# Opening the accumulators of layer 2's feed-forward by a flag instead of by products of zeros

## The chip, the cores and the metric

The kernel runs on one core of one Trainium2 chip. A core has several engines that each work through a queue of their own, in order: TensorE (PE in the profile; PEld is its weight load), VectorE (DVE), ScalarE (ACT), GpSimd (POOL) and SyncE (SP), which here issues DMAs. They meet only through semaphores. The metric is the device time of one execution in microseconds; of several runs the median is taken.

## The reference

The reference is a network of four layers on 16 sequences of 128 tokens with 128 features; each layer is an attention followed by a feed-forward, each added to x. The change lies in the feed-forward of layer 2, a product-key mixture of 1024 small experts:

```python
xn = _rmsnorm(x, norm_w)
q = (xn @ w_q.T).reshape(b, t, H, 2, DK)
sim1 = jnp.einsum('bthd,hkd->bthk', q[..., 0, :], keys[:, :, 0, :])
sim2 = jnp.einsum('bthd,hkd->bthk', q[..., 1, :], keys[:, :, 1, :])
s1, i1 = jax.lax.top_k(sim1, K)
s2, i2 = jax.lax.top_k(sim2, K)
all_idx = (i1[..., :, None] * NKEYS + i2[..., None, :]).reshape(b, t, H, K * K)
all_sc = (s1[..., :, None] + s2[..., None, :]).reshape(b, t, H, K * K)
fs, pk = jax.lax.top_k(all_sc, K)
fi = jnp.take_along_axis(all_idx, pk, axis=-1)
wd = expert_down[fi]
wu = expert_up[fi]
hidden = jax.nn.gelu(jnp.einsum('btd,bthkd->bthk', xn, wd), approximate=False)
hidden = hidden * jax.nn.relu(fs)
return jnp.einsum('bthk,bthkd->btd', hidden, wu)
```

There are H = 8 heads, 32 keys in each of two halves, and K = 8 experts are chosen per head. An expert is a pair of keys, so each token has a grid of 32 x 32 = 1024 sums of similarities per head, and the eight largest of them are wanted with their places.

## The kernel before

**No gather.** The kernel does not fetch the chosen experts. It computes the gelu for all 1024 experts and multiplies it with a weight for every expert, which is zero for those not chosen. The weight is built by subtraction. For each head the full grid C of sums is made; the eight largest are replaced in it by 0; the sum over the heads of the whole grid minus the sum of the grids with the holes leaves just the chosen sums. Both terms are gathered in one accumulator pc in PSUM, with the sign turned and turned back at the end.

**Tiles.** A tile is one sequence, 128 tokens; there are 16 (`NB`), in groups of four (`GB`). The function `layer2_ffn` is a generator whose inner functions are the steps of a tile:

- `begin(n)`, once a group: root mean square norm, transposes, `xT`, and `tT`, the similarities summed over the heads, features by tokens.
- `similar(i)`: the product psim of a tile with all keys (line 1415 copies it to `sim`).
- `thresholds(sim)`: DVE finds the eight best of each half (`best`, line 1424), POOL adds them pairwise (`sums`, line 1429), DVE finds the eight best of these (`m8`, line 1436), ACT takes relu (`out`, line 1440).
- `grid(sim, h)`: POOL adds the two halves into the 32 x 32 grid C of a head (line 1447; eight buffers C). For head 4 (`own`) ACT makes the grid row by row instead (`rows`, line 1456; buffers Cs).
- `opened(i)`: takes a new accumulator pc, two banks of 512 columns, from `ps2` (three such pairs, shared with pg of this feed-forward and pe of the attention). PE first multiplies zeros into each bank, `none` against `none`, 128 x 512 in bf16, with the start flag. Then eight products of the selection matrix `sel` with `tT` add minus the full sums, each into 128 columns, four of them per bank, without the start flag. A product of fp32 stands as two records in the profile.
- `taken(pc, h, C, m8)`: DVE searches the head's grid and puts zeros at the eight largest (line 1475), then PE transposes the grid in eight pieces onto pc (line 1477), adding.
- `gelus(i)`: PE makes pg, ACT its gelu G (line 1406).
- `weighted(pc, G)`: DVE multiplies -pc by G (line 1485), when all eight heads are in.
- `summed(i, A)`: PE multiplies G with the up-projection into po, and DVE adds it to X (line 1494).

The products made by the helper `mm` all carry line 232 in the profile, so they are told apart by their tile names; the same holds for transposes through `transposed` (line 293).

**What sets the order.** For each tile the loop writes: `opened(i)`, then for heads 0 to 7 the next tile's grids, rows and part of its thresholds and `taken`; `summed(i - 1)` stands after head 2, `gelus(i)` after head 4, `similar(i + 2)` after head 6; `weighted` ends the tile. The function `layers_1_and_2` takes one piece of this generator and one piece of the attention of layer 2 for the last two groups in turn (`chains`), so that both run side by side. In that attention line 1249 to 1263 is the softmax, line 1282 and 293 are transposes of x and E, and line 245 is the reciprocal root on POOL (`rstd`) behind which ACT scales (`low`, line 270, and x or xn, line 274). The written order is only the wish: the framework fills each engine's queue at build time by a planner that, with costs of its own for every instruction, takes among those that it believes ready the one written first. Semaphores and buffers are assigned afterwards; on the chip every queue then runs strictly as filled.

Of the kernel before, what the change touches and what calls it, by code (L numbers as in the profile page):

```python
# [19 lines left out]
P = 128  # L20
# [161 lines left out]
def build(ctx: ExitStack, tc: tile.TileContext, x, ctxt, mask, packs, cols, out):  # L182
# [45 lines left out]
    def ps2(name):  # L228
        return pss.tile([P, 2, 512], F32, tag="s", name=name)

    def mm(o, lhsT, rhs, start=True, stop=True):
        return nc.tensor.matmul(o, lhsT=lhsT, rhs=rhs, start=start, stop=stop)  # L232
# [1123 lines left out]
    def layer2_ffn(wk):  # L1356
# [8 lines left out]
        none = wk.tile([P, 512], BF16, name="none", bufs=1)  # L1365
# [94 lines left out]
        def opened(i):  # L1460

            n, b = divmod(i, GB)
            tT = group[n][1][:, b * P : (b + 1) * P]
            pc = ps2("pc")
            for r in range(2):
                mm(pc[:, r, :], none[:, :P], none, start=True, stop=False)
            for k in range(8):
                mm(pc[:, k // 4, k % 4 * P : (k % 4 + 1) * P], w["sel"][:, k * P : (k + 1) * P], tT,
                   start=False, stop=False)
            return pc  # L1470

        def taken(pc, h, C, m8):
# [39 lines left out]
        for i in range(NB):  # L1512
            pc = opened(i)
            if i % GB == 1 and i + GB < NB:
                begin(i // GB + 1)
            if i + 1 < NB:
                pieces = thresholds(sims[i + 1])
            for h in range(8):
                at = 8 * i + h + 4
                if at < 8 * NB and at % 8 != own:  # L1520
                    Cs[at] = grid(sims[at // 8], at % 8)
                if i + 1 < NB:
                    if h == 0:
                        Cs[8 * i + 8 + own] = slow()
                    rows(sims[i + 1], Cs[8 * i + 8 + own], h)
                taken(pc, h, Cs.pop(8 * i + h), m8)
                if h == 2 and last is not None:
                    summed(i - 1, last)
                if h == 4:
                    G = gelus(i)  # L1530
                if h == 6 and i + 2 < NB:
                    sims[i + 2] = similar(i + 2)
                if i + 1 < NB:
                    later = next(pieces)
                yield
            last, m8 = weighted(pc, G), later
# [171 lines left out]
```

## Time and profile before

| | us |
|---|---|
| median of 3 runs | 1429.53 |
| lowest and highest | 1420.95, 1430.63 |
| the profiled execution | 1422.77 |
| its span, from first to last instruction | 1421.0 |
| PE busy in the span | 1174.5 (83%) |
| DVE busy | 866.8 (61%) |
| ACT busy | 701.1 (49%) |
| POOL busy | 466.6 (33%) |
| mean granted clock of TensorE | 0.898 |
| 32 products of zeros, first and last start | 908.8, 1226.5 |

Times in a profile row are counted from the start of the span. A row of a group gives the line, the engine and operation, what is written from what is read, the shapes and how many there were; then the busy time and the mean of one in ns; then the idle time of the engine just before them, and who ended it. A row of the waits names who waited, for whom, the sum in us, the number of waits and the longest. A row of the order of time gives start and length in us, engine, line and operation, and in brackets the idle time before it. A row of the chain gives start, length and what ran. "issue" is time for which no waiting is seen. The length of a product includes its way through the pipeline, so two products in a row overlap; the step from one start to the next is what a product costs PE.

### The profile page before, as it was taken

Reading aid. Unit: us, or ns where it says so; the run is one execution under the profiler, and the core shown is the slowest. Engines: PE = TensorE matmul, PEld = TensorE weight load, DVE = VectorE, ACT = ScalarE, POOL = GpSimd, SP = SyncE. Lnnn points to the kernel's source line nnn. Section 1 sums busy time; section 2 is a strip of 40 time slices with the busy share of each in tenths; the row PEclk is TensorE's granted clock in tenths of the full one; section 3 lists DMA queues with packets and bytes.
Section 4 is the critical chain, followed back from the end, with each engine's and each line's share of the span. In section 5 each row is a group of like instructions: output and inputs, shape, how many; then the busy total and the mean of one; then the engine's idle time right before and its main releaser. Section 6 shows DMA issues by size and latency. Waiting matters only on the chain. (4 is left out here: it accounts for less than half of the span.)

```text
span 1421.0 us, 25103 instructions
## 1 busy us (share of the span) xinstructions
PE 1174.5 (83%) x9948; PEld 793.1 (56%) x9948; DVE 866.8 (61%) x2249; ACT 701.1 (49%) x1519; POOL 466.6 (33%) x543
## 2 busy tenths in 40 slices
PE   5887799898998877987778387568989999979996
PEld 2445355454544423455557266447868888825465
DVE  7666456565655585666554431237867999775653
ACT  4444465564665332565534146348768675334331
POOL 3213000000000045554230400229867899641100
PEclk9998799999999967899879588769999999999997
DMA  7000000000000020000012112000000000000001
GB/s 232 2 2 19 0 0 1 0 1 0 1 1 0 13 100 1 2 2 2 2 39 70 58 42 100 12 0 1 1 2 1 5 6 2 1 7 1 2 2 30
DMA packets 27590, 27.09 MB, mean 19 GB/s; under 512 B 3408, under 2 KB 25808, under 8 KB 27088
## 3 DMA queue, kind: packets, MB, share of 16 engines
q1 hardware_dynamic: 22128, 22.08, 4.7%
q0 software_dynamic: 1024, 2.10, 0.5%
q10 hardware_dynamic: 4320, 1.31, 0.4%
q8 instruction: 78, 1.28, 0.3%
q14 instruction: 40, 0.33, 0.1%
HBM read 17.88 MB, written 7.60 MB: 18 GB/s over the span
## 5 line engine op out<-in xcount | busy, mean ns | idle before, releaser
L1447 POOL TENSOR_TENSOR C<-sim 128x1024 f32<-128x1024 f32 x112 | 211.4, 1913 | 26.8 <-PE pc L1477 12.5
L232 PE MATMUL pc<-hm,weights_f 128*128 128x512 f32 x320 | 148.3, 595 | 3.0 <-DVE hm L840 2.6
L245 POOL TENSOR_TENSOR rstd<-ve,minus_half 128x4 f32<-128x4 f32 x44 | 44.9, 1020 | 292.7 <-DVE ve L242 275.4
L1475 DVE MATCH_REPLACE8 C<-out,C 128x1024 f32<-128x1024 f32 x112 | 135.0, 1208 | 0.0
L461 DVE TENSOR_REDUCE nm<-s 128x8 f32<-128x1024 f32 x96 | 114.2, 1217 | 21.2 <-PE s L232 20.5
L1477 PE MATMUL pc<-consts,C 128*128 128x128 f32 x896 | 115.9, 278 | 7.3 <-DVE C L1475 6.7
L1456 ACT ACTIVATE Cs<-sim 128x32 f32<-128x32 f32 x512 | 113.8, 310 | 1.5 <-PE pc L1477 1.2
L1477 PEld LDWEIGHTS pc<-consts,C 128*128 128x128 f32 x896 | 103.6, 144 | 15.1 <-issue 8.1
L525 DVE RECIPROCAL inv<-av 128x128 f32<-128x128 f32 x48 | 45.9, 957 | 89.0 <-PE av L232 89.0
L354 POOL MEMSET V<- 128x2560 f32 x6 | 13.4, 2258 | 248.7 <-PE pb L934 236.2
L605 ACT ACTIVATE pT<-st 128x1024 f32<-128x1024 f32 x64 | 62.3, 1022 | 66.0 <-PE st L232 66.0
L232 PEld LDWEIGHTS pc<-hm,weights_f 128*128 128x128 f32 x320 | 59.9, 190 | 55.5 <-issue 45.9
L232 PE MATMUL st<-Qb,K 32*128 32x512 f32 x512 | 82.8, 651 | 0.0
L232 PE MATMUL s<-Kb,Q 32*128 32x512 f32 x384 | 74.7, 679 | 6.5 <-ACT pT L533 2.9
L535 POOL TENSOR_TENSOR E<-pT 128x1024 f32<-128x1024 f32 x32 | 60.5, 1907 | 55.7 <-ACT pT L533 55.7
L475 POOL CAST nms<-nm 128x16 bf16<-128x16 f32 x64 | 14.6, 255 | 157.1 <-DVE nm L461 132.6
L232 PEld LDWEIGHTS av<-pT,V 128*32 128x32 f32 x1536 | 43.2, 117 | 40.4 <-issue 26.3
L533 ACT ACTIVATE pT<-st 128x1024 f32<-128x1024 f32 x32 | 31.4, 1022 | 61.6 <-PE st L232 61.5
L232 PE MATMUL av<-pT,V 128*32 128x128 f32 x1536 | 58.5, 294 | 1.6 <-DVE inv L549 1.2
L840 DVE TENSOR_TENSOR hm<-he,M 128x512 f32<-128x512 f32 x64 | 40.8, 686 | 29.9 <-ACT he L836 27.1
L232 PE MATMUL av<-pT,consts 128*32 128x128 f32 x1536 | 54.4, 283 | 0.0
L603 ACT ACTIVATE pT<-st,keys_out 128x1024 f32<-128x1024 f32 x32 | 33.9, 1111 | 37.1 <-PE st L232 37.1
(370 smaller groups left out, 2674.7 us busy)
## 6 DMA issues: line engine op xcount, KB each, us to landing
weights_f<-in_f SPq DMA_DIRECT2D x1, 3852.5 KB, 12.0
weights_f<-in_f SPq DMA_DIRECT2D x1, 2816.5 KB, 9.7
rows<-zero SPq DMA_DIRECT2D x2, 1344.0 KB, 14.9
of<-rows SPq DMA_DIRECT2D x14, 192.0 KB, 2.5
outs<-rT SPq DMA_DIRECT2D x14, 192.0 KB, 2.0
weights_f<-in_f SPq DMA_DIRECT2D x1, 2351.5 KB, 11.2
X<-in_x ACTq DMA_DIRECT2D x4, 256.0 KB, 9.5
ctx_sb<-in_ctx SPq DMA_DIRECT2D x4, 256.0 KB, 5.8
```

The source lines that it names most:

```text
L232: return nc.tensor.matmul(o, lhsT=lhsT, rhs=rhs, start=start, stop=stop)
L245: nc.gpsimd.tensor_tensor(o, ve, minus_half[:, :w], ALU.pow)
L461: nc.vector.tensor_reduce(nm[:, b, 8 * u : 8 * u + 8], ss[u].rearrange("p r (g k) -> p (r g) k", g=4), AX.X, ALU.max, negate=True,)
L525: nc.vector.reciprocal(y, s)
L535: nc.gpsimd.tensor_mul(E2, E, E)
L603: nc.scalar.activation(pT, st, AF.Exp, bias=keep[1][:, i : i + 1])
L605: nc.scalar.activation(pT, st, AF.Exp)
L840: nc.vector.tensor_mul(hm[:, k, c : c + 2, :], he, M[:, k, c : c + 2, :])
L1447: nc.gpsimd.tensor_add(C, sim[:, h, 0, :].unsqueeze(2).to_broadcast(sh), sim[:, h, 1, :].unsqueeze(1).to_broadcast(sh),)
L1456: nc.scalar.activation(C[:, k, :], sim[:, own, 1, :], AF.Identity, bias=sim[:, own, 0, k : k + 1])
L1475: nc.vector.match_replace(at, m8[:, h, :], at, 0.0)
L1477: nc.tensor.matmul(pc[:, k // 4, k % 4 * P : (k % 4 + 1) * P], lhsT=C[:, 4 * k : 4 * k + 4, :].rearrange("p i j -> p (i j)"), rhs=ident, s ...
```

## The change

In `opened`, the loop with the two products of zeros is removed. The first of the four selection products of each bank (k = 0 and k = 4) now carries the start flag; the other six go on without it. The tile `none` and the memset that fills it stay in the program, without a reader.

```diff
             pc = ps2("pc")
-            for r in range(2):
-                mm(pc[:, r, :], none[:, :P], none, start=True, stop=False)
             for k in range(8):
                 mm(pc[:, k // 4, k % 4 * P : (k % 4 + 1) * P], w["sel"][:, k * P : (k + 1) * P], tT,
-                   start=False, stop=False)
+                   start=k % 4 == 0, stop=False)
             return pc
```

## The prediction

> **What bounds the kernel now.** I first asked what the engines do in the stage that the diff touches. The table of busy time by stretch answers it (columns: PE, PEld, DVE, ACT, POOL busy with instruction counts, then granted clock, DMA share, GB/s):
>
> ```profile
> 1120.00:1160.00 40.00, 36.53 (x285) 33.53 (x286) 36.35 (x120) 30.07 (x115) 32.06 (x20) 0.96 0.03 9
> 1160.00:1200.00 40.00, 39.57 (x336) 37.28 (x335) 39.84 (x118) 24.55 (x98) 38.17 (x22) 1.00 0.01 2
> 1200.00:1240.00 40.00, 36.86 (x317) 34.91 (x315) 32.47 (x92) 14.18 (x53) 30.42 (x18) 1.00 0.00 1
> ```
>
> Three engines are nearly full at once: from 1160 to 1200 us PE 39.6, DVE 39.8 and POOL 38.2 of 40 us. Busy shares alone can't say what a shorter PE is worth here; the waits must.
>
> Next the waits, for all engines from 960 to 1240 us:
>
> ```profile
> DVE m L1436 <- POOL sums L1429: 12.6, 9, 5.2
> POOL C L1447 <- PE pc L1477: 12.5, 14, 2.4
> ...
> PE pt L1282 <- ACT x L274: 7.5, 5, 3.1
> ...
> PE po L232 <- DVE G L1485: 3.6, 3, 2.3
> ```
>
> Both directions occur: POOL waits for PE to free a buffer C (12.5 us in 14 waits), and PE waits for ACT (the attention's x) and for DVE's G. So PE is the late engine in some places and early in others. PE's order of time around a tile opening shows both:
>
> ```profile
> 1195.32 1.04 PE L1477 MATMUL pc<-consts,C 128*128 128x128 f32 x8
> 1196.20 0.59 PE L232 MATMUL pc<-none 128*128 128x512 bf16 x2
> 1196.63 1.95 PE L232 MATMUL pc<-tT,weights_f 128*128 128x128 f32 x16
> 1198.41 2.78 PE L1477 MATMUL pc<-consts,C 128*128 128x128 f32 x24
> 1203.46 2.05 PE L232 MATMUL po<-weights_f,G 128*128 128x128 f32 x16 [2.26 <-DVE G L1485]
> ...
> 1218.24 2.05 PE L232 MATMUL po<-weights_f,G 128*128 128x128 f32 x16 [0.88 <-DVE G L1485]
> ...
> 1226.28 0.59 PE L232 MATMUL pc<-none 128*128 128x512 bf16 x2
> ```
>
> The first row is the last eight transposes of tile 12; opening of tile 13 follows without a gap, then 24 transposes, and then PE stands 2.26 us for G of tile 12, although that tile's pc was complete at about 1196.2. G was simply late in DVE's queue. PE time saved between 1196 and 1201 therefore lengthens this wait and nothing else.
>
> Last, the chain that ended last. It can be followed back only to 1053 us; its pieces with an opening in them are
>
> ```profile
> 1080.52 0.65 PE pc L232 x4
> ...
> 1082.57 1.56 PE pc L232 x14
> ...
> 1196.36 2.22 PE pc L232 x18
> ...
> 1226.45 2.21 PE pc L232 x18
> ```
>
> That is three of the eleven openings after 1053 us. The other eight lie beside longer DVE, POOL or ACT work.
>
> **The change part by part.** *Removed:* two products of zeros per tile, 32 in all. The duration shown (379 ns) includes the pipeline; what counts is the step to the next start. The pair starts at 1196.20 and the first selection product at 1196.63: 0.43 us, and 0.44 at 1226.28 against 1226.72. Sixteen pairs are 16 x 0.433 = 6.9 us of PE, the most that the removal can give directly. Their weight loads (98 ns each) are beside PE.
>
> How much lies on the path? After 1053 us three openings: 3 x 0.43 = 1.3 us. The one at 1196 is doubtful (the wait at 1203 absorbs it on PE; POOL runs on without a gap), so 0.9 to 1.3. The last one is safe: from 1218.24 PE has no further gap until 1239, while POOL's last C has ended at 1230.4 and DVE stands 5.8 us for its last G. Before 1053 us the chain is not shown. Tile 0 opens at 908.8 and its first transpose starts only at 967.7, so its pair is worth nothing; the four openings from 980 to 1037 I take at the rate of the others, 3 in 11: 4 x 0.27 x 0.43 = 0.5 us (bounds 0 and 1.7). Sum: 1.3 + 0.5 = **1.8 us**; bounds with the order of instructions kept: 0.4 (only the last tile) and 6.9.
>
> *Moved:* the flag, and with it the wait for a free pair of banks, from the first product of zeros to the first selection product. No opening in the stage shows idle time ahead of it, so nothing queues behind that wait. A selection product's load (191 ns) now follows a transpose instead of a 216 ns product. The nearest row is the gelu product set behind transposes (1190.06 x8, then 1190.93: 0.87 us, 109 ns a piece, no gap), so I take 0; if the cover were gone, 191 - 109 = 0.08 us per tile, 1.3 us in all. Below nothing isn't possible, since the order of loads and products stays. The tile of zeros itself and its one memset (519 ns on POOL) stay.
>
> *A rule that speaks against it.* Work taken from PE just ahead of a wait makes PE's idle longer. Rows: from start to start PE stood 3.33 us until 1121.05, and the clock of 1118 to 1126 was 0.79; it stood 2.69 us until 1143.22 and 2.53 until 1203.46, and both stretches show 1.00. With 0.43 added the latter two become 3.1 and 3.0 us. The Trainium skill, "TensorE: Matmul & The Clock Gate", section "Why this matters for your kernels", advises against PE gaps over about 3 us, its section on what is happening gives a free-running window of about 3.4 us. By the rule's short figure both gaps may drop the clock, for one window: half of 3.4, so 1.7 us each, 3.4 us, more than the gain. By the rows and the window's length neither does (longest unpunished 2.69, punished 3.33, mine between). I take 0 because 3.0 and 3.1 are under the window, and keep 1.7 to 3.4 us for the range.
>
> *The order.* Each engine's queue is filled at build time by a planner which takes what it believes is ready. The diff changes that belief from the first opening on. DVE's G of tile 12 stands behind seven searches of tile 13, that of tile 3 behind one, so positions do move. A G one search earlier is 1.19 us earlier (searches 1212.27 and 1213.46); PE waited for G in four of the last tiles for 4.1 us, so a luckier plan can give up to that. An unluckier one is the rival below. Neither is in the trace; I take 0 and keep both ends.
>
> The profiled execution: span 1421.0, its own time 1422.77 (1.8 around the span). 1422.77 - 1.8 = 1421.0. But it lies 6.8 below the median of the three runs, 1429.53 (1420.95 to 1430.63); on the median the same saving gives 1429.53 - 1.8 = **1427.7 us**. The runs' own spread of 9.7 us is five times what I expect, so only many rounds could show it; 1% of the time, 14.3 us, is about what a measurement of this kernel can tell from no change.
>
> **The rivals.**
>
> *PE is the bound throughout.* For: PE idles almost nothing between 1144 and 1187 us, with tiles 13.64 us apart. Against: DVE is at 39.8 of 40 us there, and PE's waits for G follow. It gives 6.9: 1422.6 us. With a luckier order of G (up to 4.1 more) it reaches 1418.5.
>
> *Hidden wholly.* Only the last tile's 0.4 counts: 1429.1. For: eight of eleven openings are off the chain. It sits inside my own case.
>
> *Slower: a reshuffled POOL queue.* The two attention chains that run beside the tiles pass through POOL ten times for rstd:
>
> ```profile
> L1447 POOL TENSOR_TENSOR C<-sim 128x1024 f32<-128x1024 f32 x101 | 190.8, 1914 | 26.0 <-PE pc L1477 12.5 <-issue 5.0 <-PE pe L232 4.5
> L245 POOL TENSOR_TENSOR rstd<-ve,minus_half 128x4 f32<-128x4 f32 x10 | 10.4, 1035 | 2.6 <-ACT ve L240 1.9 <-PE pc L1477 0.7
> ```
>
> With PE believed earlier, a C buffer seems free earlier, and the planner sets one more grid C (1.87 us from start to start) ahead of an rstd. Behind an rstd stand ACT's low and x and then PE, which is in order: ACT low waits for rstd 11.1 us in 7 waits already. Price: 1.87 us for each rstd that falls behind one C more, at most 10 x 1.87 = 18.7 us. From the first that isn't made up, 1.87 - 1.8, the change no longer gains; from nine (16.8 - 1.8 = 15.0) it is over 1% slower. Half of them, my price for this case: 9.4 - 1.8 = 7.6, so 1437 us. Against it: the same shift can as well put a C behind an rstd. More table loads on ACT (1.28 us) I exclude: four loads for the exponentials and four for gelu stand beside four groups of exponentials, so they are already fully interleaved.
>
> *It doesn't do what it says.* Were the flagged product to clear only its own 128 columns, old sums would stay and the output would be wrong, at the same time of 1427.7. No trace shows this; "PSUM — Partial Sum Buffer", "The four PSUM rules", says that the flag clears the whole bank's marks, so the three unflagged products overwrite.
>
> **How the numbers follow.** Own case (0.4 to 3 us gained, order about as now) 0.55; full gain, with or without luck, 0.15; slower order 0.27, of which over 1% slower 0.1; a much luckier order of the chains 0.03. The range takes own case, full gain and most of the slower one, with the runs' spread (their low end 8.6 below the median): 1416 to 1438. Within 1% are 1415.2 to 1443.8: faster 0.05, same 0.83, slower 0.12.
>
> **What would show it.** Right: no pc from zeros; first selection product directly behind a transpose at 0.11 us; tiles in the full stretch near 13.2 us on PE but not on DVE or POOL; PE's wait for G longer (above 4.1 us); PE's last G some 0.4 to 3 us earlier in the span. The PE rival: tiles 13.2 us apart, with no more waiting for G. The slower one: ACT low's wait for rstd well above 11.1 us, and the attention ending later than 1145 us. Clock drops near 1143 or 1203 would show the rule. I am wrong if stages before 900 or after 1250 us move by more than the stage itself, or if the planner's new order moves more than 5 us.

## The result and the profile after

The change made the kernel slower: median 1434.49 us (1429.12 to 1443.36, 14 runs) against 1427.7 us before (1420.95 to 1431.33, 14 runs). The ratio is 1.0065, with a 95% interval of 1.0046 to 1.0084: between 6.6 and 12.0 us lost. It is within 1%, and inside the range, but on the other side of the 1.8 us that were forecast as a gain. All times of tiles and stretches below come from one profiled execution of each kernel; a ratio comes from many runs, each kernel against the kernel before in the same rounds. (The prediction took 1% as about the least that could be told from no change; these runs tell 0.65%.)

The products of zeros are gone (9916 records of products instead of 9948), and the profiled execution's span grew from 1421.0 to 1429.8 us. The page's first lines after the change:

```profile
span 1429.8 us, 25054 instructions
## 1 busy us (share of the span) xinstructions
PE 1174.3 (82%) x9916; PEld 794.5 (56%) x9916; DVE 864.4 (60%) x2249; ACT 703.1 (49%) x1521; POOL 465.9 (33%) x543
```

PE's busy time hardly fell (1174.5 to 1174.3) although 32 products are missing. So others must have become longer, which points at the clock: from 972 us to the end of the stage the mean granted clock is 0.99 before and 0.96 after. To find where the time went I read the start of each tile's first selection product in both traces, and cut the stage at these starts. The stage runs from the product pk with the keys (937.3 us before, 939.2 after) to the last product po (1242.5 and 1253.4):

| stretch | before | after |
|---|---|---|
| start of the stage (pk) to the last po | 305.3 | 314.2 |
| pk to tile 0 | 20.0 | 19.8 |
| tile 0 to tile 6 | 123.5 | 121.2 |
| tile 6 to tile 7 | 19.7 | 27.0 |
| tile 7 to tile 9 | 36.7 | 36.2 |
| tile 9 to the last po | 105.3 | 110.1 |
| behind the last po | 178.4 | 176.4 |

Up to tile 6 the change gains 2.3 us, which is near the forecast; but the kernel with all its zeros in the new order (below) takes 121.5 us there too, and the change in the old order 123.1, so these 2.3 us aren't the saved products. Then tile 6 alone takes 7.3 us more, and the last six tiles take 4.8 us more. The edit moves the lines behind it: what is line 1477 (transposes), 1475 (searches) and 1485 (G) in the kernel before is 1475, 1473 and 1483 after the change, and 1478, 1476 and 1486 in the first run below. This is POOL's order of time in that tile, first before, then after (start, length, engine, line, operation, and in brackets the idle time before it):

```profile
1085.14 1.92 POOL L1447 TENSOR_TENSOR C<-sim 128x1024 f32<-128x1024 f32 x1 [2.39 <-PE pc L1477]
1087.01 1.02 POOL L245 TENSOR_TENSOR rstd<-ve,minus_half 128x4 f32<-128x4 f32 x1
1088.00 3.78 POOL L1447 TENSOR_TENSOR C<-sim 128x1024 f32<-128x1024 f32 x2
```

```profile
1086.68 5.66 POOL L1447 TENSOR_TENSOR C<-sim 128x1024 f32<-128x1024 f32 x3 [2.18 <-PE pc L1475]
1092.29 1.02 POOL L245 TENSOR_TENSOR rstd<-ve,minus_half 128x4 f32<-128x4 f32 x1
1093.28 1.07 POOL L1429 TENSOR_TENSOR sums<-best 128x512 f32<-128x512 f32 x1
```

Before, one grid C stands ahead of the root; after, three. The root's input ve ends at 1088.6 us in the changed kernel, so the root lies ready for 3.7 us behind grids (0.9 before). What hangs behind it shows in the waits around tile 6, first before (1079 to 1105 us), then after (1080 to 1112 us):

```profile
PE pt L1282 <- ACT x L274: 1.7, 1, 1.7
ACT low L270 <- POOL rstd L245: 1.6, 1, 1.6
```

```profile
ACT low L270 <- POOL rstd L245: 3.8, 1, 3.8
...
PE pt L1282 <- ACT x L274: 2.9, 1, 2.9
```

and in PE's order of time, the row of pg before, then the changed kernel:

```profile
1094.30 1.95 PE L232 MATMUL pg<-xT,weights_f 128*128 128x128 f32 x16
```

```profile
1091.15 0.55 PE L1475 MATMUL pc<-consts,Cs 128*128 128x128 f32 x3 [0.20 <-DVE Cs L1473]
1094.60 1.51 PE L1282 MATMUL pt<-consts,x 128*128 128x128 f32 x4 [2.90 <-ACT x L274]
...
1099.39 3.46 PE L232 MATMUL pg<-xT,weights_f 128*128 128x128 f32 x16
```

ACT waits for the root, PE waits 2.9 us for ACT's x, and then the 16 records of pg take 3.46 us, where they took 1.95 before: the clock has been halved, from 1095.55 us on for 6.8 us. The stretches from 1094 to 1104 us, before and after, give the granted clock in the column behind POOL:

```profile
1094.00:1104.00 10.00, 10.00 (x93) 9.80 (x92) 9.13 (x30) 9.33 (x36) 6.37 (x5) 1.00 0.01 2
```

```profile
1094.00:1104.00 10.00, 9.35 (x48) 8.74 (x49) 3.51 (x13) 6.60 (x19) 2.22 (x2) 0.66 0.01 2
```

PE is nearly as busy as before by this measure (9.35 of 10 us), but with 48 records instead of 93.

### The profile page after: what moved, and what is told of

Same layout as the page of the kernel before. It is cut to its first block, busy times and chain, and to the rows that moved or that the text cites. A ratio compares the mean times of both kernels' runs of the same rounds, so it can differ in the third digit from the quotient of the medians.

```text
span 1429.8 us, 25054 instructions
## 1 busy us (share of the span) xinstructions
PE 1174.3 (82%) x9916; PEld 794.5 (56%) x9916; DVE 864.4 (60%) x2249; ACT 703.1 (49%) x1521; POOL 465.9 (33%) x543
## 5 line engine op out<-in xcount | busy, mean ns | idle before, releaser
L1473 DVE MATCH_REPLACE8 C<-out,C 128x1024 f32<-128x1024 f32 x112 | 135.1, 1208 | 0.0
L840 DVE TENSOR_TENSOR hm<-he,M 128x512 f32<-128x512 f32 x64 | 40.7, 685 | 29.9 <-ACT he L836 27.1
L232 PE MATMUL ph<-xnext,weights_f 128*128 128x256 f32 (+1 forms) x96 | 32.1, 457 | 24.1 <-DVE xnext L893 24.1
```

The costliest lines, as they stand in the source:

```text
L840: nc.vector.tensor_mul(hm[:, k, c : c + 2, :], he, M[:, k, c : c + 2, :])
L1473: nc.vector.match_replace(at, m8[:, h, :], at, 0.0)
```

## The experiments

To separate the order of the queues from the work in them, a kernel's queues can be held: for each engine a table gives the order in which its instructions stood in another build, and each instruction is tied behind its predecessor by an edge that sets order alone, with no semaphore. The diffs below leave out these tables, and what stands behind # in them is added here.

```python
...
last = None
for run in text.split():
    first, many = map(int, run.split("+"))
    for i in written[engine][first : first + many]:
        if last is not None:
            tc.add_manual_dep(i, last.name, behind, reason="held")
        last = i
```

Two theories stood against each other. *Order*: the planner's new order of the queues loses the time, as the slower rival of the prediction had it. *Chip*: the removal itself costs, through an exposed weight load (one that no longer runs beside a product), the moved wait or the clock.

### The change in the old order

Tile 0 keeps its pair, since the old order opens it 50 us ahead of its first use; the other 30 products go.

```diff
+            if i == 0:
+                for r in range(2):
+                    mm(pc[:, r, :], none[:, :P], none, start=True, stop=False)
             for k in range(8):
                 mm(pc[:, k // 4, k % 4 * P : (k % 4 + 1) * P], w["sel"][:, k * P : (k + 1) * P], tT,
-                   start=k % 4 == 0, stop=False)
+                   start=i > 0 and k % 4 == 0, stop=False)
...
+        held(tc)
```

> The change with the order of before: every engine's queue is held in the order of the kernel before, and the products of zeros are gone from tiles 1 to 15 (tile 0 keeps its pair, which lies 50 us ahead of its use). Theory 'order' (the loss is made by the new order of the queues): no loss, ratio to before 0.995 to 1.000, best guess 0.9987 (1.8 us less); tiles 13.2 to 13.6 us apart in the full stretch. Rival 'chip' (the removal itself costs, by an exposed weight load, by the moved wait or by a clock drop): as slow as the change, 1.005 to 1.008, with selection products more than 0.112 us apart or new stretches at half clock.

Measured: ratio 1.0007 (0.9993 to 1.0021), stage 305.2 us against 305.3. The loss is gone, so it came from the order. But the gain is gone too: the interval leaves at most 0.07%, 1 us, of the 1.8 that were forecast. The last selection openings show where it went; this is PE's order of time in this run:

```profile
1197.97 2.78 PE L1478 MATMUL pc<-consts,C 128*128 128x128 f32 x24
1203.45 3.40 PE L232 MATMUL po<-weights_f,G 128*128 128x128 f32 x16 [2.69 <-DVE G L1486]
...
1226.28 1.95 PE L232 MATMUL pc<-tT,weights_f 128*128 128x128 f32 x16
1228.06 2.78 PE L1478 MATMUL pc<-consts,C 128*128 128x128 f32 x24
1231.17 1.05 PE L232 MATMUL po<-weights_f,G 128*128 128x128 f32 x7 [0.33 <-DVE G L1486]
```

PE waits 2.69 us for G where it waited 2.26, and starts po at 1203.45 instead of 1203.46: the 0.43 us became a longer wait. Then the clock drops: po takes 3.40 us instead of 2.05. The stretch from 1200 to 1208 us before, with a clock of 1.00, and in this run, with 0.79:

```profile
1200.00:1208.00 8.00, 5.74 (x52) 5.50 (x51) 7.11 (x30) 3.10 (x15) 8.00 (x6) 1.00 0.00 0
```

```profile
1200.00:1208.00 8.00, 5.31 (x36) 5.07 (x34) 7.11 (x30) 3.10 (x15) 8.00 (x6) 0.79 0.00 0
```

At 1231.17 the saving of the last tile ends in a wait of 0.33 us as well: G comes when it came before.

### The old work in the new order

```diff
+        held(tc)    # the kernel before, with the tables of the changed kernel
```

> The kernel before, products of zeros included, with every queue held in the order of the changed kernel. Theory 'order': slower than before by what the change lost and by what the zeros cost on top, ratio 1.0065 to 1.012, best guess 1.008. Rival 'chip': equal to before, 0.998 to 1.002.

Measured: 1.0100 (1.0072 to 1.0128). The order alone makes the kernel with all its zeros slower, somewhat more than the change was; tile 6 takes 28.5 us. Together with the first run this decides for the order.

### One queue at a time

```diff
+        held(tc)    # the changed kernel, POOL's table alone, from before
```

> The change with POOL's queue alone held in the order of before; the other engines are planned anew around it. If the reciprocal roots set behind grids on POOL make most of the loss, ratio 0.999 to 1.002, and tile 6 takes about 20 us and not 27. If the place of G on DVE makes most of it, 1.004 to 1.007.

Measured: 0.9990 (0.9972 to 1.0009); tile 6 takes 19.0 us. DVE was planned anew and left G where the change has it, one or two searches behind in tiles 7 to 14, not three to seven as before. So the earlier G costs nothing that the runs can show, and POOL's order is enough to undo the loss.

```diff
+        held(tc)    # the changed kernel, DVE's table alone, from before
```

> The change with DVE's queue alone held in the order of before; the other engines are planned anew around it. If the place of G on DVE makes most of the loss, ratio 0.998 to 1.002 with G three to six searches behind again in tiles 9 to 14 and these tiles 13.6 to 14.5 us apart. If POOL's order makes most of it, 1.003 to 1.007.

Measured: 1.0011 (0.9998 to 1.0025). This alone would have spoken for G, but the expectation was badly posed: with DVE held, the planner also set POOL anew, and there the root of tile 6 stands behind 51 grids, as before, not 53; tile 6 takes 22.1 us. The stage of its profiled execution is 315.0 us long, as long as in the kernels that lost time, while the median of its 22 runs is not. Why that one execution stands so far off is open; the run tells nothing on G.

### One root

Only one instruction moves in POOL's queue; all queues are otherwise held in the changed kernel's order. The cuts in this part and the next ones show the queue, by what is written, and not the source.

```diff
 C<-sim
+rstd
 C<-sim
 C<-sim
-rstd
 sums<-best
```

> The change with all queues held in its own order, but the reciprocal root of tile 6's stretch (the sixth of the stage, at 1092 us) set two grids earlier on POOL, where it stood before. If this one place makes the loss of tile 6: that tile takes 19 to 22 us instead of 27.0, ACT's low waits about 1.6 us for it instead of 3.8, the half clock at 1095 to 1102 is gone, ratio to before 1.000 to 1.003. If the tile's loss has another cause: 27 us and 1.005 to 1.008.

Measured: 0.9996 (0.9974 to 1.0018). Tile 6 takes 20.9 us instead of 27.0. Moving one instruction of 1.02 us by two places removes the loss of the runs. (In the profiled execution the stage is still 308.6 us long, 3.3 more than before.) ACT's low waits 0.2 us for the root, less than expected. PE's order of time shows that it finds x ready:

```profile
1094.44 0.79 PE L1282 MATMUL pt<-consts,x 128*128 128x128 f32 x4
```

The counter-test puts the same root two grids later in the kernel before, zeros included:

```diff
 C<-sim
-rstd
 C<-sim
 C<-sim
+rstd
```

> The kernel before, products of zeros included, all queues in its own order, but the root of tile 6's stretch set two grids later on POOL, as the new order has it. If that place alone costs what tile 6 lost: tile 6 takes 24 to 28 us instead of 19.7, ratio 1.003 to 1.006. If it costs only with the rest of the new order: 19 to 21 us, ratio 0.999 to 1.001.

Measured: 1.0028 (1.0011 to 1.0044), a little below the expected span, and tile 6 takes 27.1 us instead of 19.7. So this root alone costs some 4 us in the old order, while moving it back in the new order won some 10 (1.0065 to 0.9996); why it weighs more there is open. PE stands 4.39 us for x and the clock falls to half for the ten microseconds behind:

```profile
1094.84 1.51 PE L1282 MATMUL pt<-consts,x 128*128 128x128 f32 x4 [4.39 <-ACT x L274]
```

```profile
1094.00:1104.00 10.00, 9.16 (x36) 7.64 (x37) 3.88 (x15) 5.61 (x21) 2.50 (x2) 0.50 0.01 2
```

### Another root

The last six tiles lost 4.8 us in the profile after. There the root of layer 3's first norm stands six grids earlier than before. All queues held in the changed kernel's order, this root was moved back.

```diff
-rstd
 C<-sim
...
+rstd
```

> The change with all queues held in its own order, but the root of layer 3's first norm, which floats into the stage at 1189 us, set six grids later on POOL, where it stood before. If its wait on POOL makes the loss of the last six tiles: from the opening of tile 9 to the end of the stage 105 to 107 us instead of 110.1, ratio 1.002 to 1.005. If the early place of G on DVE makes it: 110 us and 1.005 to 1.008.

Measured: 1.0061 (1.0039 to 1.0082), no better than the change; the last stretch takes 108.5 us instead of 110.1, less of a gain than expected. This root isn't the cause. The one-root run above has this long last stretch too (110.7 us), although its runs lose nothing measurable. In the changed kernel PE waits there for POOL's grids, which it did not before. The waits of PE from 1140 to 1254 us begin with the first row; the second is its wait for G, 4.1 us in the kernel before:

```profile
PE pc L1475 <- POOL C L1447: 5.3, 4, 2.1
...
PE po L232 <- DVE G L1483: 0.5, 1, 0.5
```

Why POOL is late there was not tried and stays open.

### The clock behind the wait

To price the clock alone, PE was kept busy in the wait of tile 6: twelve products of zeros into the bank that the transposes overwrite, all queues held in the changed kernel's order.

```diff
+        calls = []
...
             pt = ps1("pt")
+            calls.append(x)
+            for _ in range(12 if len(calls) == 7 else 0):
+                mm(pt, identb, nought.to_broadcast([P, GT]))
```

> The change with all queues held in its own order, and 12 products of zeros of 128 x 512 in bf16 (some 2.6 us of PE) set on PE just ahead of the transposes of x in tile 6, where PE stands 2.9 us; they write a bank that the transposes overwrite. If the half clock behind that wait is part of the loss: no half clock at 1095 to 1102, tile 6 takes 23 to 25 us instead of 27.0, ratio to before 1.002 to 1.005. If the clock follows and costs nothing on the path: 27 us, 1.005 to 1.008.

Measured: 1.0014 (0.9998 to 1.0029), a little better than expected; tile 6 takes 24.0 us instead of 27.0. The rows of PE, and the clock of the stretch from 1094 to 1104 us:

```profile
1094.97 2.77 PE L232 MATMUL pt<-nought,identb 128*128 128x512 bf16 x12
1098.03 1.37 PE L1287 MATMUL pt<-consts,x 128*128 128x128 f32 x4 [0.29 <-ACT x L274]
...
1101.29 2.03 PE L232 MATMUL pg<-xT,weights_f 128*128 128x128 f32 x16
```

```profile
1094.00:1104.00 10.00, 9.46 (x63) 6.68 (x62) 5.42 (x16) 6.74 (x20) 5.66 (x4) 1.00 0.01 2
```

The root is as late as in the change, but the clock stays whole. The runs gain more than this tile does (1.0065 to 1.0014 is some 7 us, by the intervals 2.4 us at least), which a single profile doesn't explain. In these four executions the 7.3 us of tile 6 split into 3.0 us for the clock (27.0 - 24.0), 3.1 us for the late root itself (24.0 - 20.9), and 1.2 us for something else in the new order (20.9 - 19.7). The first share fits the trace: 6.8 us at half clock cost at most 3.4.

### Roots set early, without and with the zeros

If a root's place is worth so much, there should be more to win. Starting from POOL's old order, three other roots that had waited for grids were set one, two and one grids earlier; the other engines were planned anew, as in the run with POOL's old order alone (0.9990).

One of the three:

```diff
-C<-sim
 rstd
+C<-sim
```

> The change with POOL's queue in the order of before, and in it three roots of the attention set earlier by one, two and one grids (the fourth, seventh and ninth of the stage, which waited 3.0, 3.8 and 2.3 us with their input there); the other engines are planned anew. If each grid fewer ahead of a root is worth some 1.9 us on the path: ratio 0.994 to 0.998, faster than both. If the path lies elsewhere by then: 0.998 to 1.001.

Measured: 0.9936 (0.9914 to 0.9958), median 1417.62 us: faster than both kernels. The stage takes 297.1 us, and over 960 to 1240 us

```profile
ACT low L270 <- POOL rstd L245: 7.4, 7, 2.1
```

where it was 11.1 us before. No wait of PE for ACT's x exceeds 1.2 us here, where the longest was 3.1, and from 972 us to the end of the stage the clock never drops (1.00), while the kernel before has two stretches of 3.4 us at half clock. How much of the gain is the roots' own and how much the clock's was not separated. Now the same order with the zeros back in:

> The kernel before, products of zeros included, with all queues held in the order that the run with three roots set earlier had (0.9936 there without zeros). If the gain of that run is the order's alone, the zeros being hidden as in the first run: ratio 0.993 to 0.995. If with a shorter path PE's 6.9 us begin to count: 0.996 to 0.999.

```diff
+        held(tc)    # the kernel before, with the tables of the run above
```

Measured: 0.9934 (0.9917 to 0.9950), stage 297.7 us. In this order too the zeros cost nothing that the runs can show, and the 6.9 us of PE's time, 0.5%, would have shown; the stages differ by 0.6 us in one execution each.

## Why the prediction was wrong, point by point

**The sum of the removal.** "3 x 0.43 = 1.3 us" and "0.5 us" before 1053 us, 1.8 in all, was wrong; with the order kept it is nothing that the runs can show (1.0007, and 0.9936 against 0.9934). The pair's 0.43 us was right, its place on the path was not. The chain names for each step one releaser; that an opening is on it doesn't say by how much the next one was later. Even the opening called safe, that of tile 15, wasn't: PE had no gap behind it until 1239 us, but DVE's G arrived at the same moment as PE did, so that 0.44 us saved turned into a wait of 0.33. The bound "with the order of instructions kept: 0.4" should have been 0.

**The order, taken as 0.** This is the step that turned the sign. The rival "a reshuffled POOL queue" described what happened: more grids ahead of a root, ACT's low and x and then PE behind it, at 1.87 us a grid. (That a freed C was believed earlier is the prediction's account of the planner; no run here looks into it.) It was priced for half of the ten roots, and one was enough: two grids more ahead of the root of tile 6. Of the ten, one other fell behind two grids more, the third, and the run with one root moved keeps it there without a loss; four were set earlier. (The last of the ten isn't the attention's, but layer 3's.) The price for one was too low: 2 x 1.87 = 3.7 us is near the 3.1 us of the late root itself, but the half clock behind it wasn't in the sum. Its first mark was only half right: the wait of low for rstd over the whole stage moved little, 11.1 to 11.4 us, as other roots were luckier; the one in tile 6 went from 1.6 to 3.8. The second, the attention ending later than 1145 us, depends on where one ends it: its last write to X ended at 1139.3 us instead of 1137.1, but the transposes of the xn made from it start at 1148.6 instead of 1143.2.

**The clock, taken as 0.** The Trainium skill's page "TensorE: Matmul & The Clock Gate" was weighed at the right place and discarded on a wrong reading of the rows. The prediction took 2.69 us from start to start as unpunished and 3.33 as punished, and compared gaps with the window's length. The kernel before has both outcomes for the same gap:

```profile
1054.38 0.33 PE L293 MATMUL pt<-consts,x 128*128 128x128 f32 x1 [2.43 <-ACT x L274]
...
1143.22 0.33 PE L293 MATMUL pt<-consts,xn 128*128 128x128 f32 x1 [2.42 <-ACT xn L274]
```

```profile
1052.62:1056.03 3.41, 1.65 (x12) 1.22 (x13) 2.84 (x14) 2.52 (x9) 1.13 (x2) 1.00 0.00 0
1056.03:1059.44 3.41, 3.41 (x9) 1.69 (x8) 1.38 (x3) 1.19 (x3) 2.92 (x3) 0.50 0.00 0
1141.37:1144.78 3.41, 1.56 (x14) 1.46 (x15) 3.41 (x13) 2.85 (x11) 3.41 (x3) 1.00 0.00 0
1144.78:1148.20 3.42, 3.42 (x26) 2.80 (x25) 2.22 (x7) 3.42 (x13) 3.42 (x3) 1.00 0.02 7
```

So the length of a gap alone doesn't decide. In each of the twelve traces the stretches at half clock start on one grid of 3.41 us and last one step of it or several, which agrees with the page's section "What's actually happening": it gives a free-running window of about 3.4 us. What goes with a drop is how busy PE was in the step just ended. From 900 to 1260 us the twelve traces have 1020 such steps at full clock: all 81 in which PE was busy for less than 43% were followed by half clock, 5 of the 20 between 43% and 50%, and none of the 919 above. (The two shown lie in between: 48% was followed by a drop, 46% was not; what decides there is open.) A whole idle window isn't needed. In the first run, PE was busy for 1.27 us of the step from 1199.49 to 1202.90, 37%, and the half clock began at 1202.90, while PE still waited; before, it was 1.81 us of the step from 1199.39, 53%. But the 2.26 us of idle time that went unpunished there dropped the clock in the run with the root set later (1213 us), so that the 0.43 us made the difference isn't shown. In the first run the drop cost the path nothing (stage 305.2 us against 305.3), since PE was waiting anyway. In tile 6, where PE had become the late one, it cost 3.0 us.

**G's place on DVE.** The prediction held that a luckier place of G could give up to 4.1 us. G did move earlier by two to five searches in tiles 9 to 14, and PE's waits for it fell from 4.1 to 0.5 us. Nothing came of it: in that stretch PE waited 5.3 us for POOL's grids instead, and with POOL's old order held, where it waited 1.0 us for them, the runs gained nothing measurable either (0.9990).

**What held.** The flag does what it says: the output is right without the zeros. In 12 of the 15 tiles from 1 on the first selection product starts 0.109 to 0.110 us behind a transpose (in tiles 4, 5 and 7 another product stands ahead of it), so the exposed load of 0.08 us that was bounded does not exist. The stages ahead of this one and behind it moved by 2 us each, in opposite directions.

**More table loads** had been excluded, and that was wrong: ACT has 1521 instructions against 1519, and the two more are table loads, 11 in the stage instead of 9. So the groups could still be split further. They don't make the loss, though: the run with one root moved has the same 11 and no loss.

## What to carry to other kernels

Removing work from one engine also changes what a planner believes, and the new order of all queues can cost more than the work was worth. Hold the old order and measure the removal by itself before judging it, and compare where the small instructions on which a serial chain hangs stand in a queue of long ones: here one root of 1 us among grids of 1.9 us decided some 10 us in one order and 4 in another, and setting three others earlier, with the waits and clock drops that went with it, gave 0.64%. Time saved on an in-order engine counts only if it is still the later one at its next wait; look for the tie, not for the gap.

## What the runs showed of the hardware that was not expected

An idle time of PE well below 3 us can halve the clock, and one as long can leave it whole: 2.43 us of idle time at 1054 us in the kernel before dropped it for 3.4 us, 2.42 us at 1143 us did not; 2.79 us did not in the change, and did in the run with one root moved. In all twelve traces the drop goes with how busy PE was in the step of a fixed grid of 3.41 us that had just ended: below 43% always, above 50% never. The grid doesn't start with the kernel: counted from the span's start, its steps begin 1.3 us past a multiple of 3.41 in the kernel before, 3.3 in the change and 3.0 in the run with one root moved. So the same wait can drop the clock in one execution and not in another, and one trace doesn't say how often it does.

Products of zeros in the wait keep the clock whole: with twelve of them, 2.6 us of PE's time, tile 6 was 3.0 us shorter, and the ratio went from 1.0065 to 1.0014. In this kernel zeros that nobody needed cost nothing in one place, and were useful in another.
